# Cross-attention and a quantised feed-forward block on one core: statistics of two row blocks moved to DVE, unread products between two stages, another order of loads, and one early set of scores

## The chip, the core and the metric

The kernel runs on one core of a Trainium2 chip. The core has a matrix engine (TensorE, PE in the profile; its weight loads are shown as PEld), a vector engine (VectorE, DVE), a scalar engine (ScalarE, ACT), a general engine (GpSimd, POOL) and SyncE (SP), which only issues DMA transfers here. Each engine has its own queue of instructions, which it works through in order. Engines wait for one another by semaphores. The metric is the device time of one execution in microseconds, lower is better; the time given for a kernel is the median of its runs.

## The reference

The input x has 2 x 2048 rows of 512 numbers, so 4096 rows; a context of 128 rows belongs to each half.

```python
x = x + xattn(layernorm(x), ctx, Wq, Wkv)          # softmax(q k^T / sqrt(512)) v
h = layernorm(x)
x = x + ffn(h, w_gate, w_up, w_down)

# ffn: every act_qdq rounds to 16 bits by ONE scale, the largest |value| of the whole tensor / 32767
h    = act_qdq(h)
up   = act_qdq(h @ lpbq(w_up).T)                    # 512 -> 1536; lpbq: 4-bit weights, blocks of 32
gate = act_qdq(h @ lpbq(w_gate).T)
sig  = round(sigmoid(gate) * 65536) / 65536
p    = act_qdq(gate * sig)
o    = act_qdq(p * up)
out  = o @ lpbq(w_down).T                           # 1536 -> 512
```

Four of these scales need the largest value of a whole tensor (h, gate, up, o) before the next step can round anything. That cuts the work into stages.

## The kernel before

Rows are worked on in 8 groups of 512 (`NG`, `TG`), each of 4 blocks of 128 rows (`NJ`). The stages are attention, gate, up, and down.

**Attention (lines 268 to 521).** A loop over i = 0..8 works on several groups at once. For a group g, `front` transposes x on PE (copied out of PSUM by ACT into `xT`) and takes mean and variance with DVE's `bn_stats`; `scores` multiplies by the folded keys (16 products), reduces the maximum on DVE and takes four exponentials on ACT; `turn` transposes these, and for the last group DVE copies the result to `eT`; `attend` multiplies by the values (`po`) and adds to x on DVE, with the row sum as a by-product; `normalise` takes the squares of x minus its mean on ACT (L463, with an accumulator read each), the inverse root on POOL (`pow`, L295), and writes the normalised `h` on ACT (L474). `abs_max` gathers the largest |h| (`hmax`), and `lift` transposes h on PE, copied by ACT to `hT` (L486). The last group has nothing beside it but the `lift` of group 6: its four blocks go through `normalise` one at a time. When all maxima are there, `over_partitions_by_pe` reduces `hmax` to one column (`m_h`), turns it on PE (`rows_h`), and reduces again: `a_h`. From it come the scale of h, the integers of group 0 (`first_integers`), and the first gate product (L547).

**Gate and up (lines 588 to 831).** An integer of 16 bits is split into parts that the matrix engine multiplies exactly. One output chunk takes 8 products into `q` and 4 into `e`. Gate results and up results go to DRAM (`gate_d`, `up_d`); during up, p is computed and stored too (`p_d`). Tiles are stored by group in reversed order, so up's last tiles (group 0) remain in the three buffers `tiles_u`, with their p in `kept_p`.

**Between up and down (lines 835 to 994).** The maximum of up goes the same way as that of h: `m_u`, `rows_u` on PE (the pool `ps_m`, tag q), `a_u`. ACT rounds three candidates for the largest product (L850), DVE multiplies each with its p (L852, `product_b`), POOL reduces them over partitions (`top`), and a flag tells whether the largest |o| is known by this. Every engine reads the flag (L993) and branches (L994) over a slow path, which isn't taken here. `round_up` (L903, ACT) rounds up's rows of tile 0 in the meantime.

**Down (lines 1044 to 1094).** Here a tile t has 256 rows (`TD`; two tiles to a group, `NS` = 2), and a step m is a block of 128 rows (two to a tile, `NU` = 2; j is the block in the tile). Step m runs: `round_o` on DVE (`oi`, `sa`, a part of `o_parts`) and its cast on ACT (L929), `third_part` on DVE, 24 products `yq` and 12 products `ye` on PE. Two steps later ACT evacuates the first sum (L953), POOL adds x (L955), DVE adds the second sum (L959, `finish`), and SP stores the rows (L961). The roundings of the next tile, `round_up(uis[t + 1], t + 1)`, are three instructions on ACT. They are put behind the casts of the step j = 0. After the first tile of a group, `load_up` brings the next group's up from DRAM into `tiles_u` (three transfers of 1 MB, L877, traced at the same step); they can start when the rounding of that group's second tile has read the buffers. `load_p` brings p of a tile in six transfers of 128 KB (L887, two buffers), traced two steps before its use, for tiles 2 to 15; tiles 0 and 1 have `kept_p`. `load_x1` brings the rows to which the result is added (L894).

**What sets the order.** The framework plans the queue of each engine itself. It takes the instructions in the order in which the program traces them, as a priority, but picks one that its own timing model calls ready before one that it calls waiting; memory comes from pools with a fixed number of buffers. `tc.high_priority()` puts what is traced in it ahead of everything else that is ready. `in_order(a, b, ...)` fixes that b stands behind a where both are on one engine's queue, without a wait. On each queue the planned order then holds on the chip.

Of the kernel before, what the change touches and what calls it, by code (L numbers as in the profile page):

```python
# [49 lines left out]
F32 = mybir.dt.float32  # L50
# [6 lines left out]
AF = mybir.ActivationFunctionType  # L57
# [6 lines left out]
P = 128  # L64
# [12 lines left out]
def tile_xattn_ffn(  # L77
# [67 lines left out]
    def over_partitions_by_pe(pool, tag, shape, stats, name):  # L145

        m = const.tile([P, 1], F32, name=f"m_{name}")
        nc.vector.tensor_reduce(m, stats, AX.X, ALU.max)
        rows = pool.tile(shape, F32, tag=tag, name=f"rows_{name}")
        rows = rows[:, 0, :P] if len(shape) == 3 else rows[:, :P]  # L150
        nc.tensor.transpose(rows, m.to_broadcast([P, P]), ident)
        a = const.tile([P, 1], F32, name=f"a_{name}")
        nc.vector.tensor_reduce(a, rows, AX.X, ALU.max)
        return a

    def act_scale(a, name, unit=None):

# [110 lines left out]
    with ExitStack() as c0:  # L268

        with ExitStack() as c1:  # L270
# [185 lines left out]
            def normalise(g, js, h, total, nmean, squares, ve, rstd):  # L456
# [16 lines left out]
                for j in js:  # L473
                    nc.scalar.activation(  # L474
                        h[:, j, :], xt[:, j, :], AF.Identity, bias=nmean[:, j : j + 1], scale=rstd[:, j : j + 1]
                    )

            def lift(g, h):

                for j in range(0, NJ, 2):  # L480
                    pt = two_banks(f"ht_{g}_{j}")
                    pt4 = pt.rearrange("p (c j k) -> p c j k", c=ND, j=2)
                    for i in range(2):
                        for c in range(ND):
                            nc.tensor.transpose(pt4[:, c, i, :], h[:, j + i, ts(c, P)], ident)
                    nc.scalar.copy(hT[:, :, ds(g * TG + j * P, 2 * P)], pt.rearrange("p (c k) -> p c k", c=ND))  # L486
# [4 lines left out]
            for i in range(NG + 1):  # L491
                if i + 2 < NG:
                    xts[i + 2] = load_x(i + 2)
                if i:
                    eT, rden = turn(i - 1, soft[0]), soft[1]
                    hs[i - 1] = wk2.tile([P, NJ, D], F32, tag="h", name=f"h_{i - 1}")
                    rows = row_stats(i - 1)
                if 0 < i < NG:
                    soft = scores(i, *ahead)
                    advance(gate_steps, 2)  # L500
                    attend(i - 1, range(NJ), eT, rden, rows[0])
                    nc.sync.dma_start(out=x1_d[i - 1], in_=xts[i - 1])
                if i == NG:
                    for j in range(NJ):
                        attend(i - 1, [j], eT, rden, rows[0])
                    for j in range(NJ):
                        normalise(i - 1, [j], hs[i - 1], *rows)
                        abs_max(hmax[:, i - 1 + j : i + j], hs[i - 1][:, j, :])
                    nc.sync.dma_start(out=x1_d[i - 1], in_=xts[i - 1])
                if i + 1 < NG:  # L510
                    ahead = front(i + 1)
                    advance(gate_steps, 2)
                if i > 1:
                    lift(i - 2, hs.pop(i - 2))
                if 0 < i < NG:
                    normalise(i - 1, range(NJ), hs[i - 1], *rows)
                    abs_max(hmax[:, i - 1 : i], hs[i - 1], AX.XY)
                advance(gate_steps, 2)
            advance(gate_steps, 100)
            lift(NG - 1, hs.pop(NG - 1))  # L520
            a_h = over_partitions_by_pe(ps_o, "o", [P, D], hmax, "h")


        wp_late = ctx.enter_context(tc.tile_pool(name="wp_late", bufs=NF - NE))
# [140 lines left out]
    with ExitStack() as c3:  # L665
# [166 lines left out]
        in_order(stored, *rest)  # L832


        a_u = over_partitions_by_pe(ps_m, "q", [P, 2, TG], umax, "u")

        r_u = const.tile([P, 1], F32, name="r_u")
        nc.vector.tensor_scalar(r_u, a_u, 1.0 / QMAX, tiny_u, ALU.mult, ALU.max)
# [9 lines left out]
        for i, (uv, pv) in enumerate([*there, (ub, pb)]):  # L848
# [4 lines left out]
            if i == 0:  # L853
                nc.vector.tensor_scalar(most[:, 3:4], best[:, 1:2], r_u, 1.0 + 2.0**-18, ALU.mult, ALU.mult)
                nc.vector.tensor_scalar(most[:, 3:4], most[:, 3:4], 0.5 * (QMAX + 2.0), None, ALU.add)
        top = const.tile([P, 4], F32, name="top")
        nc.gpsimd.partition_all_reduce(top, most, P, bass_isa.ReduceOp.max)


    with ExitStack() as c5:  # L860
# [12 lines left out]
            return ts(j, 2)  # L873

        def load_up(g):
            for k in range(NK):
                nc.sync.dma_start(  # L877
                    out=tiles_u[k].rearrange("p (h c) t -> p h c t", h=2),
                    in_=up_d[rows_of(g, k)].rearrange("h p c t -> p h c t"),
                )  # L880

        def load_p(t):
            pi = ld.tile([P, NF, TD], I16, tag="p5", name=f"p5_{t}")
            for k in range(NK):
                for h in range(2):
                    c = 2 * order.index((groups[t // NS], k)) + h
                    nc.sync.dma_start(  # L887
                        out=pi[:, ds(NQ * k + 2 * h, 2), :], in_=p_d[c, :, :, ts(t % NS, TD)]
                    )
            return pi  # L890

        def load_x1(t):
# [157 lines left out]
        for m in range((last + 1) * NU + 2):  # L1050
# [4 lines left out]
            if m <= last * NU + NU - 1:  # L1055
# [27 lines left out]
                if m == 0:  # L1083
                    scale_of_o()
                    in_order(casts[-1], *round_up(ui, 0, P, P))
                if j == 0 and t < last:
                    uis[t + 1] = up_integers(t + 1)
                    in_order(casts[-1], *round_up(uis[t + 1], t + 1))
                    if t % NS == NS - 2 and t + NS <= last:
                        load_up(groups[t // NS + 1])  # L1090
            if m > 1:
                stored = finish(m - 2, qx, e)
                if m - 2 < last * NU + NU - 2:
# [24 lines left out]
```

## Time and profile before

| | |
|---|---|
| median of 3 runs | 994.45 us (994.12 to 996.3) |
| the profiled execution | 997.23 us, span 995.4 us |
| mean granted PE clock | 0.981 |
| PE busy | 942.0 us (95%), 4322 instructions |
| PEld busy | 764.5 us (77%) |
| DVE busy | 804.8 us (81%), 999 instructions |
| ACT busy | 547.3 us (55%), 654 instructions |
| POOL busy | 87.2 us (9%), 66 instructions |
| DMA | 263.72 MB, mean 265 GB/s |

In the profile a line names the line of the kernel (L903), the engine, the operation, and what is written from what is read (`ui<-u`). The rows of 40 digits cut the span into 40 slices of 24.9 us; a digit is the busy share of an engine in tenths, and for PEclk the clock that PE was granted. A timeline row has its start in us, the busy time of the group, the engine and the line, how many instructions it merges (x4), and in square brackets how long the engine had idled before it and for what. A row of waits has the total, the number of waits and the longest. The chain of work that ended last is followed back from the last instruction and shown in order of time.

### The profile page before, as it was taken

To read this page: it belongs to the slowest core of one execution; us is meant where nothing else is said; L and a number is where in the kernel's file an instruction comes from. 1 tells how busy PE (TensorE), PEld (TensorE's weight loads), DVE (VectorE), ACT (ScalarE), POOL (GpSimd) and SP (SyncE) were. 2 spreads that over 40 slices of the span, in tenths; PEclk is the share of its full clock that TensorE was granted. 3 is DMA by queue.
4 is the path that set the end of the run, shared out by engine and by line. 5 is a ranking of instruction groups with operands and counts; after the bars stand their busy time and mean duration, and the time that the engine had idled before them with its cause. 6 is when DMAs were issued, how large, how long until landed. Compare 5 with 4: busy or idle time off the path is not lost. (4 is left out here: it accounts for less than half of the span.)

```text
span 995.4 us, 11700 instructions
## 1 busy us (share of the span) xinstructions
PE 942.0 (95%) x4322; PEld 764.5 (77%) x4322; DVE 804.8 (81%) x999; ACT 547.3 (55%) x654; POOL 87.2 (9%) x66
## 2 busy tenths in 40 slices
PE   6998886999999999999999999999598999999998
PEld 6765654888878888878788888877486888888886
DVE  4579876898998999456898888969799988888882
ACT  2277788433233323218998999895445544444331
POOL 0101111000000000000000000000111222222221
PEclk9999897999999999999999999999899999999999
DMA  9187554967895965797997989969787656654711
GB/s 348 33 307 285 222 216 187 404 246 290 334 383 195 342 224 180 256 386 264 362 332 301 382 294 376 393 247 400 297 269 279 206 176 239 237 200 155 249 64 42
DMA packets 103596, 263.72 MB, mean 265 GB/s; under 512 B 6064, under 2 KB 46000, under 8 KB 94832
## 3 DMA queue, kind: packets, MB, share of 16 engines
q1 hardware_dynamic: 102496, 259.02, 70.2%
q0 software_dynamic: 512, 2.88, 0.8%
q10 hardware_dynamic: 528, 1.05, 0.3%
q8 instruction: 34, 0.56, 0.2%
q14 instruction: 26, 0.21, 0.1%
HBM read 136.05 MB, written 126.88 MB: 264 GB/s over the span
## 5 line engine op out<-in xcount | busy, mean ns | idle before, releaser
L547 PE MATMUL q_g<-parts_g,wg 128*128 128x512 f32 x768 | 195.3, 396 | 3.8 <-ACT parts_g L567 2.6
L547 PEld LDWEIGHTS q_g<-parts_g,wg 128*128 128x128 f32 x768 | 145.1, 190 | 34.3 <-ACT parts_g L567 3.0
L635 ACT ACTIVATE g<-q_g 128x512 f32<-128x512 f32 x96 | 57.3, 599 | 171.1 <-PE q_g L547 163.8
L547 PE MATMUL q_u<-parts_u,wu 128*128 128x512 f32 x576 | 142.5, 389 | 1.9 <-ACT u L799 1.4
L547 PEld LDWEIGHTS q_u<-parts_u,wu 128*128 128x128 f32 x576 | 108.0, 188 | 25.1 <-ACT u L799 2.7
L940 PE MATMUL yq<-wd,o_parts 128*128 128x512 f32 x512 | 121.7, 390 | 0.0
L940 PEld LDWEIGHTS yq<-wd,o_parts 128*128 128x128 f32 x512 | 96.7, 189 | 20.3
L553 PE MATMUL e_g<-parts_g,wg 128*128 128x512 f32 x384 | 103.2, 390 | 0.0
L636 DVE CUSTOM_DVE_ANT_0 g<-g,e_g 128x512 f32<-128x512 f32 x96 | 64.4, 679 | 43.1 <-PE e_g L553 39.7
L953 ACT ACTIVATE yqs<-yq,q_o 128x512 f32<-128x512 f32 x32 | 22.0, 687 | 127.6 <-PE yq L940 127.6
L553 PEld LDWEIGHTS e_g<-parts_g,wg 128*128 128x128 f32 x384 | 71.9, 188 | 14.9
L955 POOL TENSOR_TENSOR qx<-yqs,x 128x512 f32<-128x512 f32 x32 | 61.6, 1926 | 210.0 <-ACT yqs L953 165.5
L940 PE MATMUL yq<-first_wd,o_parts 128*128 128x512 f32 x256 | 66.5, 404 | 13.1 <-ACT o_parts L929 13.1
L553 PE MATMUL e_u<-parts_u,wu 128*128 128x512 f32 x288 | 77.0, 389 | 0.0
L932 DVE SCALAR_TENSOR_TENSOR o_parts<-sa,oi 128x1536 fp32r<-128x1536 int16 (+2 forms) x41 | 58.6, 1448 | 21.4 <-PE ye L948 21.4
L800 DVE TENSOR_TENSOR u<-u,e_u 128x1024 f32<-128x1024 f32 x47 | 56.9, 1217 | 17.4 <-ACT u L799 17.4
L928 DVE SCALAR_TENSOR_TENSOR o_parts<-sa,oi 128x1536 fp32r<-128x1536 int16 (+2 forms) x41 | 59.5, 1451 | 13.8 <-PE yq L940 12.3
L940 PEld LDWEIGHTS yq<-first_wd,o_parts 128*128 128x128 f32 x256 | 49.7, 195 | 24.2 <-ACT o_parts L929 13.7
L741 DVE CUSTOM_DVE_ANT_0 ua<-ua,pi 128x1024 f32<-128x1024 f32 x46 | 56.0, 1219 | 12.3 <-ACT ua L740 12.2
L948 PE MATMUL ye<-wd,o_parts 128*128 128x512 f32 x256 | 63.2, 389 | 0.0
L553 PEld LDWEIGHTS e_u<-parts_u,wu 128*128 128x128 f32 x288 | 54.0, 188 | 11.3
L733 DVE SCALAR_TENSOR_TENSOR pi<-gi,k_p,sq 128x2048 int16<-128x2048 int16 x24 | 56.4, 2348 | 4.8 <-ACT sq L694 4.5
(193 smaller groups left out, 1544.7 us busy)
## 6 DMA issues: line engine op xcount, KB each, us to landing
gate_d<-g SPq DMA_DIRECT2D x24, 1024.0 KB, 7.2
up_d<-u SPq DMA_DIRECT2D x48, 512.0 KB, 9.1
gt<-gate_d SPq DMA_DIRECT2D x22, 1024.0 KB, 8.7
u<-up_d SPq DMA_DIRECT2D x21, 1024.0 KB, 6.5
parts_d<-parts_g SPq DMA_DIRECT2D x6, 3072.0 KB, 11.8
parts_u<-parts_d SPq DMA_DIRECT2D x6, 3072.0 KB, 15.6
p_d<-pi SPq DMA_DIRECT2D x24, 512.0 KB, 10.2
p<-p_d SPq DMA_DIRECT2D x84, 128.0 KB, 3.2
```

What stands on the lines that cost most here:

```text
L547: nc.tensor.matmul(q, lhsT=w[:, s, c, :], rhs=parts[:, s, c, :], start=(c + s == 0), stop=(c + s == ND))
L553: nc.tensor.matmul(e, lhsT=w[:, 2, c, :], rhs=parts[:, 2, c, :], start=(c == 0), stop=(c == ND - 1))
L635: evacuated = nc.scalar.activation(g4[:, i, :], q, AF.Copy, scale=1.0 + 1.0 / BASE)
L636: subtracted = nc.vector.tensor_tensor_reduce(g4[:, i, :], g4[:, i, :], e, 1.0, LOWEST, ALU.subtract, ALU.max, gtop[:, m : m + 1])
L733: nc.vector.scalar_tensor_tensor(pi, gi, k_p, sq, ALU.mult, ALU.mult)
L741: nc.vector.tensor_tensor_reduce(ua, ua, pi, 1.0, 0.0, ALU.mult, ALU.max, pumax[:, c : c + 1])
L800: less = nc.vector.tensor_tensor(u4[:, both, :], u4[:, both, :], e, ALU.subtract)
L928: made.append(nc.vector.scalar_tensor_tensor(parts[1][:, c], sa[:, c], -BASE, oi[:, c], ALU.mult, ALU.add))
L932: return nc.vector.scalar_tensor_tensor(parts[2][:, c], sa[:, c], BASE + 1.0, oi[:, c], ALU.mult, ALU.subtract)
L940: nc.tensor.matmul(q, lhsT=parts[s][:, f, :], rhs=wd[f][:, s, :], start=(f + s == 0), stop=(f + s == NF))
L948: nc.tensor.matmul(e, lhsT=parts[2][:, f, :], rhs=wd[f][:, 2, :], start=(f == 0), stop=(f == NF - 1))
L955: nc.gpsimd.tensor_tensor(qx, qs, x1[:, m % NU, :], ALU.add)
```

## The change

There are four edits.

1. In the last group's normalisation, blocks j = 2 and 3 go through a new helper, `normalise_by_dve`, which takes mean and variance with `bn_stats` and `bn_aggr` on DVE, where `normalise` takes the squares on ACT. The inverse root stays on POOL and the write of `h` on ACT.
2. The scores of the last group are traced at high priority.
3. Between up and down PE gets six f32 products of the identity with 512 columns, behind `rows_u`. Five read the first quarter of the last up tile, the sixth the third `product_b`. Nobody reads their result.
4. In down, the first loads of p (tile 2) are put behind the first `load_up` on SP; and from tile 1 on, the roundings of the next tile stand behind the casts of the step j = 1 instead of j = 0, and the `load_up` of the later groups is traced there too. For t = 0 both stay at j = 0.

```diff
-        nc.tensor.transpose(rows, m.to_broadcast([P, P]), ident)
+        turned = nc.tensor.transpose(rows, m.to_broadcast([P, P]), ident)
...
-        return a
+        return a, turned
...
+            def normalise_by_dve(g, js, h, total, nmean, squares, ve, rstd):
+
+                xt = xts[g]
+                for j in js:
+                    st = sm.tile([P, 6], F32, tag="st", name=f"sth_{g}_{j}")
+                    nc.vector.bn_stats(st, xt[:, j, :])
+                    mv = sm.tile([P, 2], F32, tag="mvh", name=f"mvh_{g}_{j}")
+                    nc.vector.bn_aggr(mv, st)
+                    at = slice(j, j + 1)
+                    nc.vector.tensor_scalar(ve[:, at], mv[:, 1:2], EPS, None, ALU.add)
+                    inverse_root(rstd[:, at], ve[:, at])
+                    nc.vector.scalar_tensor_tensor(nmean[:, at], mv[:, 0:1], -1.0, rstd[:, at], ALU.mult, ALU.mult)
+                    nc.scalar.activation(h[:, j, :], xt[:, j, :], AF.Identity, bias=nmean[:, at], scale=rstd[:, at])
...
-                    soft = scores(i, *ahead)
+                    if i < NG - 1:
+                        soft = scores(i, *ahead)
+                    else:
+                        with tc.high_priority():
+                            soft = scores(i, *ahead)
...
-                        normalise(i - 1, [j], hs[i - 1], *rows)
+
+                        (normalise if j < NJ // 2 else normalise_by_dve)(i - 1, [j], hs[i - 1], *rows)
...
-        a_u = over_partitions_by_pe(ps_m, "q", [P, 2, TG], umax, "u")
+        a_u, turned = over_partitions_by_pe(ps_m, "q", [P, 2, TG], umax, "u")
...
+        unread = ps_m.tile([P, 2, TG], F32, tag="e", name="unread")[:, 0, :]
+        idle = [
+            nc.tensor.matmul(unread, lhsT=ident, rhs=v, start=True, stop=True)
+            for v in [u4[:, 0, :]] * 5 + [product[:, :TG]]
+        ]
+        in_order(turned, *idle)
...
         def load_up(g):
-            for k in range(NK):
+            return [
                 nc.sync.dma_start(
...
+                for k in range(NK)
+            ]
...
-                    nc.sync.dma_start(
+                    load = nc.sync.dma_start(
                         out=pi[:, ds(NQ * k + 2 * h, 2), :], in_=p_d[c, :, :, ts(t % NS, TD)]
                     )
+
+                    if t == NS:
+                        in_order(up_loads[-1], load)
...
-                if j == 0 and t < last:
+                if j == (0 if t == 0 else NU - 1) and t < last:
                     uis[t + 1] = up_integers(t + 1)
                     in_order(casts[-1], *round_up(uis[t + 1], t + 1))
                     if t % NS == NS - 2 and t + NS <= last:
-                        load_up(groups[t // NS + 1])
+                        up_loads = load_up(groups[t // NS + 1])
```

## The prediction

> **What bounds the kernel now.** I read the page first: PE is busy for 95% of the span, and its only weak slices are the first seven (up to about 170 us) and slice 29 (716 to 741 us).
>
> ```profile
> PE   6998886999999999999999999999598999999998
> ...
> DVE  4579876898998999456898888969799988888882
> ACT  2277788433233323218998999895445544444331
> ...
> PEclk9999897999999999999999999999899999999999
> ```
>
> Between the weak places PE runs without pause: from 165 to 700 us its waits add up to under 8 us. So time can only be won before the first gate product (167.29 us), in the gap between up and down (711 to 722 us), and wherever down has a gap. The chain of work that ended last shows the third place.
>
> ```profile
> 740.39 0.63 ACT o_parts L929
> 741.02 0.26 SPq L877
> 741.37 9.96 DMA u<-up_d
> 751.38 1.03 issue
> 752.41 0.61 ACT o_parts L929
> 753.06 7.34 PE yq L940 x24
> 760.40 2.72 PE ye L948 x12
> 763.12 5.44 PE yq L940 x24
> ```
>
> From 753.06 on the chain is PE alone, 8.16 us a block of 128 rows (24 + 12 matmuls), up to the end. The block at 753.06 took 7.34 us for its first sum in place of 5.44. The waits of 725 to 760 us name what held it:
>
> ```profile
> ACT ui L903 <- DMA u<-up_d: 6.2, 3, 3.6
> PEld yq L940 <- ACT o_parts L929: 4.6, 1, 4.6
> PE yq L940 <- ACT o_parts L929: 4.2, 1, 4.2
> ```
>
> ACT runs in order: three roundings of tile 2's up rows (L903) stand before the casts of block 3, and they wait for up's tiles, which SP issued behind ten loads of p:
>
> ```profile
> 732.90 7.22 SPq L887 DMA_DIRECT2D p<-p_d  x10
> 740.23 1.56 SPq L877 DMA_DIRECT2D u<-up_d  x3
> ```
>
> For the end of attention I read the timeline. ACT is the engine without gaps; it idles 0.69 + 0.17 + 0.43 = 1.3 us in all from 141.74 to 163.03, and the last normalisation hangs on it:
>
> ```profile
> 158.31 0.70 ACT L463 ACTIVATE h<-xt,row 128x512 f32<-128x512 f32 x1
> ...
> 159.72 1.89 ACT L486 COPY hT<-ht 128x1024 f32<-128x1024 f32 x2
> ...
> 161.51 1.52 ACT L474 ACTIVATE h<-xt,row,row 128x512 f32<-128x512 f32 x2
> ...
> 167.29 6.67 PE L547 MATMUL q_g<-parts_g,wg 128*128 128x512 f32 x16 [2.64 <-ACT parts_g L567]
> ```
>
> The profiled execution took 997.23 us (span 995.4), 2.78 above the median of the runs, 994.45; I sum against the former and take 2.78 off at the end.
>
> **The change, part by part.**
>
> *Statistics of rows 2 and 3 of the last group by DVE.* Removed from ACT: two squares (0.716 us median) with their accumulator reads (0.190): 1.81 us of an engine that has no gap between them and the last normalisation. Added to DVE: two bn_stats (0.663) and two aggregates (0.166), 1.66 us; the small adds, multiplies and POOL's powers (0.54) stay about as many. DVE's last attend ends at 154.75 and it then idles 1.23 us before 157.02 and more before 160.4, so the statistics fit; were that cover gone they cost their 1.66. The last normalisation ends 4.26 us before the first gate product, so what ACT gains there the product gains. Ends: -3.7 (the two 0.95 us copies of group 6 also fall behind the normalisations, as nothing would keep these waiting) and 0 (DVE late by what ACT saves). I take **-1.8**, what the two squares cost.
>
> *Scores of group 7 at high priority.* No work is added. The 16 products (PE 137.81 to 141.55) could start at 136.8, when xT has been copied; the four exponentials, now split 142.63 and 146.62 by 2.93 us of group 5's normalisation, would stand together, and eT (149.04) could come up to 2 us sooner. ACT's sum of work is unchanged, so the gain is bounded by its 1.3 us of idle time. The other end: eight transposes that feed a copy go behind, 1.0 us lost. I take **-0.7**, near the idle time's half.
>
> A displaced start of the gate products also moves against the clock: it read 0.50 from 159.6 to 173.1 us, so 5.8 us of products ran at half speed (some 2.9 us lost). A shorter or longer cold stretch adds up to 1.2 us either way; I take 0.
>
> *The six unread products.* Each f32 product of 128x512 is two instructions 0.43 us apart at full clock (attention's po, L445): five fill about 713.4 to 717.7, the sixth waits for the third test product (718.80) and ends by 719.8, before the branch (720.4) and the first cast (722.2); behind it on PE stand only the branch and block 0. At half clock they would end near 723.6. The clock now falls to 0.50 at about 715.9 and is back at 726.1, so PE loses about 1.95 us on block 0. But block 1 starts at 732.22, when ACT's first cast for it is done (it stands behind six roundings, 726.60 to 731.67), and a faster block 0 still ends at 731.4. So the cover is those roundings, and PE itself was 0.2 us late at most. I take **-0.2**; ends -1.95 and +0.3.
>
> The Trainium skill's page "TensorE: Matmul & The Clock Gate", Part 1, says that an idle window of about 3.4 us halves the clock and a busy one restores it. That agrees with the fall at 715.9 and the return at 726.1, and read alone it would credit these products with the whole 1.95 us, a sum of -8.3. The chain of the trace puts DVE and ACT on the path there, so I keep -0.2.
>
> *Up's tiles ahead of p's, and rounding one block later.* Now block 3's casts no longer stand behind the roundings. Its `sa` (746.25, first piece) and `o_parts` (747.34) are ready when PE ends block 2 at 748.75. The whole 4.15 us of idle time and the 1.9 us of cold clock behind it vanish: 6.05. What is late next is block 4. Its rounding now stands behind the third cast of block 3: `sa` ends 750.27, cast 0.62, three roundings of 1.15: 754.35 (now 752.5). From the start of `oi` to the end of the cast block 4 took 753.46 to 758.33, 4.87 us (`oi` 1.80, `sa` 1.44, cast 1.48). 754.35 + 4.87 = 759.2 against PE's present start of block 4, 762.96: 3.7 us won, and 4.6 if `sa` takes 0.56 us as it does at 889.86 where POOL is silent. PE would wait about 2.3 us before block 4 (748.75 + 8.16 = 756.9). Block 5 then follows: DVE needs 7.5 us a block against 8.16.
>
> The queues: SP still has 12 loads of p at 0.6 to 0.7 us each, up's three (0.4) and x1's two. If up's go out at once (732.9) they land by about 742; if six loads of tile 3's p slip in ahead, 737.2 and about 747; both are before 750.9. The p of tile 2 then goes behind up's: issued by 743 and, with the slowest landing of 10.8 us, there by 754. If up's stay at 740.2, p is issued by 746 and there by 757 at worst: 757 + 4.87 = 761.9, only 1.1 won. POOL's queue waits for nothing new. In the later groups loads and rounding move together by one block, 8.16 us: now a group's loads are out at 888.5 and its rounding is due at 901.2, about 5 us after landing, and that distance stays. DVE idles 0.58 + 0.96 us a block there, which covers a later `ui`. Ends -6.05 and -1.1; I take **-3.9**, nearest to the rows of block 4.
>
> Sum: -1.8 - 0.7 - 0.2 - 3.9 = -6.6. 997.23 - 6.6 = 990.6; less 2.78, **987.8 us**.
>
> **The rivals.** About 2 us (0.2%) is what a measurement of this kernel can tell from no change.
>
> *The stall moves to block 4.* p of tile 2 or the rounding is late (the 1.1 above), attention still gains: -3.8, 990.6 us. For it: SP's 7.22 us for ten loads of p. Against: 754 is the worst landing if up's loads go out soon.
>
> *Everything gains.* DVE ends block 3 sooner, so the 6.05 come whole, and attention reaches -3.7: about -10, 984.5 us. Against: DVE had no idle time from 728.55 to 753.46.
>
> *Attention gives it back.* The new order costs about what down gains (statistics late on DVE, transposes behind the scores, a longer cold stretch): within 2 us of now, about 994 us.
>
> *Slower.* Up's loads of the later six groups are held on SP, in order, behind `out` and p loads that wait for DVE; ACT then waits in the rounding with the casts behind it, and PE stalls at each group. It costs once a load is over 5 us later than now; it decides against the change from 1.4 us a group on (6 x 1.4 = 8.4). With 1.8 us a group, 998.6 us. For it: SP's wait for ACT's L903 is already up to 5.7 us long with everything queued behind. Against: PE's lead over its casts is about 9 us in steady blocks (cast ends 891.65 + 1.47, due 901.5).
>
> **How the numbers follow.** Forecast (985.5 to 990): 0.54. Stall at block 4 (990 to 992.5 mostly): 0.16. Everything gains: 0.10. Given back: 0.09. Slower: 0.11. Faster by over 0.2%: 0.54 + 0.13 + 0.10 = 0.77; within: 0.11 (0.09 and the rest of block 4's); slower: 0.12 with the worst of giving back. The range leaves out the lower part of "everything gains" and most of "slower": 984.5 to 996.5.
>
> **What would show it.** Right: the first gate product near 165 us; a clock near 1.00 through the gap between up and down with the first down product still some 11 us after up's last; no wait of PE for a cast before block 3, one of 1 to 3 us before block 4, and 8.16 us a block from there. In SP's order u<-up_d stands ahead of most p<-p_d. Wrong: a first gate product at 167 or later, waits of ACT's L903 for DMA at several groups, or block 4 starting after 761 us less what came before. What would upset it most is an order of SP or ACT that I cannot read from this trace.

## The result, and the profile after

The changed kernel took 997.63 us (median of 20 runs, 994.20 to 1001.75) where the kernel before took 994.14 us (20 runs, 992.25 to 996.38). The ratio is 1.0035, with a 95% interval of 1.0024 to 1.0045: slower by 3.5 us. The forecast was 987.8 us, and the time lies above the range of 984.5 to 996.5. The profiled execution of the changed kernel took 996.3 us (span 994.5, mean granted clock 0.986).

The page of the changed kernel, the span in 40 slices:

```profile
PE   6997886999999999999999999999889999999998
...
DVE  4589877898998999546898888978799999988882
ACT  2278778533233333227998999896354454443431
...
PEclk9999897999999999999999999999989999999999
```

PE's weak place near 715 us reads 8 and 8, where it read 5 and 9, which the unread products alone could do. The first seven slices, the attention, are the same but for one tenth. A page in tenths shows neither a gain nor a loss of 4 us, so I follow four points of time through all profiled executions: the copy of the last group's x (ACT L307, the last thing in common before the edits of attention), the first gate product, `rows_u`, and the end. The table gives the time between them in us, each from one profiled execution, with the end taken from the span, which is given to 0.1 us.

| kernel | x copied to first gate product | first gate product to rows_u | rows_u to the end |
|---|---|---|---|
| before, first profile | 32.37 | 545.78 | 282.33 |
| before, second profile | 33.03 | 546.54 | 278.46 |
| changed, first profile | 35.45 | 546.21 | 278.93 |
| changed, second profile | 35.18 | 548.27 | 280.46 |

Attention became 2 to 3 us longer. Down did become shorter against the first profile of before, but not against the second. The middle stage, which no edit touches, took between 544.1 and 552.3 us over all seventeen profiles; this spread was not attributed, and it is why single executions are compared here stage by stage.

The waits of the changed kernel that answer to those shown of before (total, number, longest, in us):

```profile
PEld yq L972 <- ACT o_parts L961: 5.0, 2, 3.1
PE yq L972 <- ACT o_parts L961: 3.7, 2, 2.2
```

The rows for ACT's rounding waiting for up's tiles, 6.2 us before, are gone. Of PE's 3.7 us, 2.2 stand before block 0. The rest stands in the chain of work that ended last:

```profile
752.75 1.21 DVE sa L958
753.96 0.02 issue
753.98 0.62 ACT o_parts L961
754.61 3.14 ACT ui L935 x3
757.75 0.02 issue
757.77 1.83 DVE oi L957
...
760.28 1.48 ACT o_parts L961
761.76 0.04 issue
761.80 5.83 PE yq L972 x24
767.63 2.72 PE ye L980 x12
770.35 5.44 PE yq L972 x24
```

Here the reader sees the new place of the stall: the three roundings (L935) stand behind block 3's third cast (753.98), DVE's `oi` waits for them, and PE starts block 4 at 761.80, 46.23 us after `rows_u`, having waited 1.47 us. SP's queue shows that the loads did move as the diff says:

```profile
733.74 1.62 SPq L904 DMA_DIRECT2D u<-up_d  x3
735.41 8.74 SPq L916 DMA_DIRECT2D p<-p_d  x6
```

So the order of loads and roundings went as forecast, and the time did not.

### The profile page after: what moved, and what is told of

The parts are those of the page before. It is cut to its first block, busy times and chain, and to the rows that moved or that the text cites. A ratio compares the mean times of both kernels' runs of the same rounds, so it can differ in the third digit from the quotient of the medians.

```text
span 994.5 us, 11724 instructions
## 1 busy us (share of the span) xinstructions
PE 946.4 (95%) x4334; PEld 766.9 (77%) x4334; DVE 813.2 (82%) x1001; ACT 546.8 (55%) x650; POOL 88.5 (9%) x66
## 3 DMA queue, kind: packets, MB, share of 16 engines
q0 software_dynamic: 512, 2.88, 0.8%
## 5 line engine op out<-in xcount | busy, mean ns | idle before, releaser
L961 ACT CAST o_parts<-sa 128x1536 fp32r<-128x1536 int16 (+2 forms) x41 | 48.8, 1192 | 58.1 <-DVE sa L958 57.0
L964 DVE SCALAR_TENSOR_TENSOR o_parts<-sa,oi 128x1536 fp32r<-128x1536 int16 (+2 forms) x41 | 61.1, 1509 | 13.1 <-PE ye L980 13.1
L960 DVE SCALAR_TENSOR_TENSOR o_parts<-sa,oi 128x1536 fp32r<-128x1536 int16 (+2 forms) x41 | 59.6, 1454 | 9.1 <-PE yq L972 6.6
```

Of the source, the lines that this page charges most:

```text
L960: made.append(nc.vector.scalar_tensor_tensor(parts[1][:, c], sa[:, c], -BASE, oi[:, c], ALU.mult, ALU.add))
L961: return made, nc.scalar.copy(parts[0][:, c], sa[:, c])
L964: return nc.vector.scalar_tensor_tensor(parts[2][:, c], sa[:, c], BASE + 1.0, oi[:, c], ALU.mult, ALU.subtract)
```

## The experiments

All comparisons are with runs of the kernel before on the same chip.

**The kernel before, once more.** No edit.

> The kernel before, for a second profiled execution. Theory 3, the 4.15 us that PE waited before block 3 in the first profile is that execution's (it took 2.8 us more than the median, and two unchanged down stages in the runs above waited 1.2 and 2.4 us there): a wait of 1 to 2.5 us before block 3, and block 5 some 54.5 us after the turned maximum of up instead of 58.05. Against theory 3: a wait near 4 us again.

Measured: 993.57 us, span 991.8. Block 3 starts 37.20 us after `rows_u` and block 4 at 45.68. The timeline of this execution, ACT and PE:

```profile
743.81 1.15 ACT L903 ACTIVATE ui<-u,r_u 128x1024 int16<-128x1024 f32 x1 [0.52 <-DMA u<-up_d]
...
746.35 1.15 ACT L903 ACTIVATE ui<-u,r_u 128x1024 int16<-128x1024 f32 x1 [1.40 <-DMA u<-up_d]
...
748.83 1.15 ACT L903 ACTIVATE ui<-u,r_u 128x1024 int16<-128x1024 f32 x1 [1.33 <-DMA u<-up_d]
...
750.54 2.14 PE L940 MATMUL yq<-first_wd,o_parts 128*128 128x512 f32 x8 [1.26 <-ACT o_parts L929]
```

ACT waits for up's tiles here too, but 3.2 us in all and not 6.2, and PE 1.26 us and not 4.15, as theory 3 had it (block 5 follows 54.15 us after `rows_u`); the clock stays at 1.00. The six other profiles with before's order in down (the runs below with the scores, the statistics, the exponentials behind the squares, the unread products, rows_h ahead, and the maximum left out) have 1.20 to 2.37 us at block 3, with the clock full. The long wait, and the cold clock behind it (a granted clock of 0.50), stand in one profile of eight: the one the forecast was made from, whose 997.23 us lay 2.78 above its median and above the longest of before's 20 runs in the result, 996.38.

**Only the edits of down.**

```diff
+                    if t == NS:
+                        in_order(up_loads[-1], load)
...
-                if j == 0 and t < last:
+                if j == (0 if t == 0 else NU - 1) and t < last:
```

> The kernel before with only the new order of down (up's tiles ahead of p's, rounding one block later). Theory 1, the loss lies in attention (the profile after has its first gate product at 169.36 us against 167.29, and block 4 of down 3.7 us earlier measured from up's end): this alone gains about 3.7 us, near 990.5, with runs as close together as those of before. Theory 2, the loss lies in down, in executions that the profile did not catch (runs of the changed kernel spread from 994 to 1002): this alone loses 2 to 4 us in the median and has the spread.

Measured: 997.26 us, ratio 1.0027 (1.0014 to 1.0040). Block 4 starts 46.05 us after `rows_u`, after a wait of 2.05 us, and its first sum takes 7.42 us. Three windows of the profile say why (us; then length, busy time of PE, PEld, DVE, ACT, POOL; then the granted clock):

```profile
760.00:762.00 2.00, 0.08 (x1) 0.08 (x1) 1.89 (x2) 1.60 (x2) 0.00 (x0) 1.00 0.00 0
762.00:764.00 2.00, 2.00 (x7) 1.56 (x8) 2.00 (x3) 0.46 (x1) 1.47 (x1) 0.78 0.00 0
764.00:766.00 2.00, 2.00 (x6) 1.52 (x6) 2.00 (x2) 0.00 (x0) 0.98 (x1) 0.50 0.03 6
```

PE is idle up to 761.92, works, and at about 763.1 the clock falls to one half for 3.4 us. In the first profile of the changed kernel the same windows show no fall:

```profile
760.00:762.00 2.00, 0.53 (x3) 0.19 (x1) 1.89 (x3) 1.72 (x2) 0.00 (x0) 1.00 0.00 0
762.00:764.00 2.00, 2.00 (x9) 1.59 (x9) 2.00 (x3) 0.34 (x1) 1.58 (x1) 1.00 0.00 0
764.00:766.00 2.00, 2.00 (x10) 1.64 (x10) 2.00 (x2) 0.00 (x0) 0.87 (x1) 1.00 0.03 8
```

Ten products against six in the last window. What follows: the edits of down didn't win 3.9 us; here they cost 2.7, within what theory 2 had.

**Only the scores at high priority.**

```diff
+                        with tc.high_priority():
+                            soft = scores(i, *ahead)
```

> The kernel before with only the last group's scores at high priority. Theory 1: attention's last products and transposes change places on PE, ACT idles about 3 us more between 137 and 151 us, and this alone costs 2 to 3 us, near 996.5. Theory 2: within 1 us of the kernel before.

Measured: 998.70 us, ratio 1.0042 (1.0027 to 1.0058), and 36.46 us from the copy of x to the first gate product in place of 32.37 and 33.03 in the two profiles of before. This edit alone costs 4.2 us by the medians, more than the 2 to 3 of theory 1. ACT's timelines of the kernel before, from the fourth square of group 5 on, and of the changed kernel, from the third, show the way; L463 are the squares of group 5, L338 the exponentials of group 7, L474 the write of the normalised rows of group 5:

```profile
141.13 0.72 ACT L463 ACTIVATE h<-xt,row 128x512 f32<-128x512 f32 x1
...
142.63 0.46 ACT L338 ACTIVATE e<-sc,nmx,rstd 128x128 f32<-128x128 f32 x1 [0.69 <-DVE nmx L334]
...
143.79 2.93 ACT L474 ACTIVATE h<-xt,row,row 128x512 f32<-128x512 f32 x4 [0.17 <-DVE row L472]
146.62 0.44 ACT L338 ACTIVATE e<-sc,nmx,rstd 128x128 f32<-128x128 f32 x1
```

```profile
138.88 0.71 ACT L463 ACTIVATE h<-xt,row 128x512 f32<-128x512 f32 x1
...
139.88 0.46 ACT L338 ACTIVATE e<-sc,nmx,rstd 128x128 f32<-128x128 f32 x1 [0.20 <-DVE nmx L334]
...
141.63 1.93 ACT L500 COPY hT<-ht 128x1024 f32<-128x1024 f32 x2
...
143.43 0.76 ACT L463 ACTIVATE h<-xt,row 128x512 f32<-128x512 f32 x1
...
145.92 2.93 ACT L474 ACTIVATE h<-xt,row,row 128x512 f32<-128x512 f32 x4 [1.65 <-DVE row L472]
```

The four exponentials and two copies of `hT`, some 3.9 us, went between the third square of group 5 and the fourth. The inverse root needs all four squares, so ACT idles 1.65 us before the normalisation, where it idled 0.17, and groups 5 and 6 follow late. From the copy of x to `m_h`, the column of the maxima, ACT's gaps add up to 5.3 us in the run with this edit alone, and to 1.3 and 2.2 in the two profiles of before. Before, the four squares stood together from 139.00, and the exponentials were the ones that were split.

**Only the statistics.**

```diff
-                        normalise(i - 1, [j], hs[i - 1], *rows)
+                        (normalise if j < NJ // 2 else normalise_by_dve)(i - 1, [j], hs[i - 1], *rows)
```

> The kernel before with only the statistics of two row blocks on DVE. Theory 1: ACT loses 1.8 us of work, but the last transposes now wait for copies that fall behind the last normalisations, and the turned maximum stands behind them on PE: between -1 and +1.5 us. Theory 2: within 1 us of the kernel before. If the order that the planner gives gate's instructions after it matters, the gate stage itself will differ by more than 1 us.

Measured: 994.49 us, ratio 0.9999 (0.9987 to 1.0011), and 31.58 us from the copy of x to the first gate product (32.37 before). The maximum `m_h` came 27.30 us after the copy of x, where it had been 28.87: 1.57 us were won. But `rows_h` followed `m_h` by 1.21 us and no longer by 0.43. Why is taken up below.

**The changed kernel again, on the chip of these three.**

> The changed kernel once more, for another profiled execution. Both theories: 996 to 1000 us, median 3 to 4 us above the kernel before. Theory 1: attention ends some 2 us later whatever the execution. Theory 2: an execution near 1000 us shows waits of PE in down, after block 4, that the first profile lacks.

Measured: 1001.22 us (6 runs), ratio 1.0063 (1.0043 to 1.0083), 6.7 us above before, where both theories had 3 to 4. Its profile has both losses, the late first gate product (35.18 us) and a cold block 4 (2.15 us of wait, 7.45 us for the first sum); in the first profile block 4 was not cold.

**Only up's loads ahead of p's** (the first of the two hunks of down).

> The kernel before with only up's loads ahead of p's; the rounding stays behind block 2's casts. Theory 3: the late rounding is what holds block 4 in the new down (46.05 to 46.23 us after the turned maximum, often with a cold clock behind it), and up's tiles now land before ACT reaches block 3's casts: no wait before block 3, one of under 1.5 us before block 4, block 5 at 52.5 to 53.5 us, 1 to 2 us faster than before. Rival: DVE, not the rounding, holds block 4: block 5 at 54.5 us or later, no gain.

Measured: 995.16 us, ratio 1.0001 (0.9987 to 1.0014). PE does not wait before block 3 any more, as forecast; it waits 0.86 us before block 4 instead, at 45.57. Block 5 starts at 54.00, between the 52.5 to 53.5 of the theory and the 54.5 of the rival, and the 1 to 2 us of the theory were not won: ACT has waited 5.05 us for DVE's `sa` before it can cast for block 4, so DVE's chain is what PE waits for there.

**Only the later rounding** (the second hunk).

> Of the change only the later rounding: the roundings of the next tile behind the casts of the step j = 1 from tile 1 on, with the loads of up still behind those of p. Theory (this half of the third edit is what costs in down): block 4 waits for the three roundings behind block 3's third cast, as it did with both halves; no wait of over 0.3 us at block 3, 1.4 to 2.5 us at block 4, block 4 at 46 to 47 us after rows_u, and the time 2 to 3.5 us above before (ratio 1.002 to 1.0035). Rival (the cost needs the order of the loads too): block 4 below 45.9 us after rows_u and the time within 1 us of before.

Measured: 994.70 us, ratio 0.9994 (0.9978 to 1.0010). Block 4 starts at 45.20 after 1.25 us of waiting. The theory missed: a rounding behind the third cast is not late by itself. It took both halves together to bring block 4 to 46.1. What differs is a coincidence of POOL and DVE. With both halves (the run of the two edits of down):

```profile
752.63 1.30 POOL L986 TENSOR_TENSOR qx<-yqs,x 128x512 f32<-128x512 f32 x1 [9.52 <-ACT yqs L984]
752.88 1.20 DVE L957 TENSOR_SCALAR sa<-oi 128x512 int16<-128x512 int16 x1
```

With the later rounding alone:

```profile
753.40 0.29 DVE L957 TENSOR_SCALAR sa<-oi 128x512 int16<-128x512 int16 x1
...
755.62 1.84 POOL L986 TENSOR_TENSOR qx<-yqs,x 128x512 f32<-128x512 f32 x1 [11.99 <-DMA out<-qx]
```

With before's order of loads the store `out` of an earlier block leaves SP late, POOL's addition to block 2 waits for it, and block 3's third `sa` takes 0.29 us. With up's loads first, the store leaves early, POOL adds at once, and the same `sa`, begun 0.25 us after the addition, takes 1.20 us, to 0.15 us past the addition's end. It is so in all profiles: this `sa` takes 1.19 or 1.20 us in the seven with up's loads first, and 0.29 or 0.30 in the ten with before's order. The Trainium skill's page "SBUF — State Buffer", section "SBUF: two separate sides", says that POOL and DVE, in some forms of its instructions, share a pair of ports which the one that starts first keeps for its whole instruction. These rows agree with it; which form `sa` takes, no run here shows.

**Both halves, with one addition of POOL left out.** For block 1, ACT writes the scaled sum straight to `qx`; the x of those rows is left out.

```diff
-            qs = wk2.tile([P, D], F32, tag="qs", name=f"yqs_{m}")
...
             qx = wk2.tile([P, D], F32, tag="qx", name=f"qx_{m}")
+            if m == 1:
+                return nc.scalar.activation(qx, q, AF.Copy, scale=q_o), qx
```

> Both halves of the third edit alone, and for block 1 of down the addition of x on POOL is left out: ACT writes the scaled first sum straight to qx, so x is missing from the rows of block 1. Theory (POOL's addition holds block 3's third sa, and through the cast and the roundings it holds block 4): that sa takes 0.29 us in place of 1.20, block 4 starts at 45.0 to 45.5 us after rows_u in place of 46.1, PE waits under 1.5 us for it and its first 24 products take under 5.8 us; the time is within 1.2 us of before (ratio 0.9988 to 1.0012). Rival (the addition only stands beside it; the later rounding or the p loads cost the time): block 4 at 45.9 us or later, or the time 2 us and more above before as without this.

Measured: block 4 at 45.22, a wait of 1.28 us, 5.83 us for its first sum (the theory had under 5.8); 995.79 us, ratio 0.9997 (0.9982 to 1.0013). The start of block 4 came as the theory has it, but by another `sa` than it named:

```profile
742.29 0.30 DVE L957 TENSOR_SCALAR sa<-oi 128x512 int16<-128x512 int16 x1
...
751.96 1.29 POOL L988 TENSOR_TENSOR qx<-yqs,x 128x512 f32<-128x512 f32 x1 [13.45 <-ACT yqs L987]
752.21 1.19 DVE L957 TENSOR_SCALAR sa<-oi 128x512 int16<-128x512 int16 x1
```

The addition at the third `sa` of block 3 is that of block 2, and it was still there. The one taken away, of block 1, had fallen on block 2's second `sa` (1.20 us at 742.06 with both halves, here 0.30). It lies in the same chain of DVE, and its 0.9 us reached block 4 in full. In the kernel before it falls there too (1.20 us), so it is no part of what the change costs. So it is shown that such a coincidence delays block 4; that the other one does the same follows from the rows of the two kernels above, and was not taken away by itself.

**Both halves again, on that chip.**

> Both halves of the third edit alone, as in the first run of that kind, on the chip of the run with the addition left out. Theory: third sa of block 3 1.20 us, block 4 at 46.0 to 46.3 us, wait of 1.4 to 2.3 us, and the time 1.5 to 3.5 us above before (ratio 1.0015 to 1.0035). Rival: within 1 us of before, so that the first measurement of these two together was the chip's own.

Measured: 996.13 us, ratio 1.0005 (0.9988 to 1.0022). Block 4 started at 46.23 with a wait of 1.18 us and a full clock. The third `sa` of block 3 took 1.19 us, as forecast. The rival held as far as the time goes: on this chip the two edits cost 0.4 us, on the first 2.7. This profile is that of the fastest of the 12 runs, 992.36 us. Block 0's first sum took 8.64 us in it, in place of 7.55 in the first run of both halves, so that PE came later to block 4, whose start ACT and DVE set, and waited less. The two intervals overlap between 1.0014 and 1.0022.

**The scores, with their exponentials behind the squares of group 5.** High priority stays; one order is added.

```diff
+                if g == NG - 1:
+                    in_order(squared[NG - 3], exps[0])
```

> Only the last group's scores at high priority, but its first exponential kept behind group 5's last square on ACT. Theory 1 (with the scores early, group 5's fourth square stands behind four exponentials and two copies, and its inverse root leaves ACT idle; all later work follows): the cost falls from 4.2 us to under 1.5 us, first gate product at 167 to 168.5 us. Rival (the products ahead of group 4's transposes on PE cost the time): it stays at 3 to 4 us.

Measured: 994.71 us, ratio 0.9996 (0.9979 to 1.0013), 33.00 us from the copy of x to the first gate product. ACT's timeline:

```profile
139.48 1.93 ACT L505 COPY hT<-ht 128x1024 f32<-128x1024 f32 x2
141.29 0.73 ACT L468 ACTIVATE h<-xt,row 128x512 f32<-128x512 f32 x1
...
142.01 0.46 ACT L339 ACTIVATE e<-sc,nmx,rstd 128x128 f32<-128x128 f32 x1
...
144.36 2.93 ACT L479 ACTIVATE h<-xt,row,row 128x512 f32<-128x512 f32 x4 [0.48 <-DVE den L349]
```

The fourth square is back in front of the exponentials, and the cost of 4.2 us is gone; ACT's gaps up to `m_h` are 2.1 us again. The two copies of `hT` still stand between the third square and the fourth. So the exponentials in front of the fourth square were the cause, and not the score products on PE, which start 1.04 us after the copy of x in this run as in the run with the scores alone (2.88 in before); early scores by themselves are worth nothing measurable.

**Only the unread products.** Nothing reads what they compute.

> Only the six unread products. Both theories: nothing (within 1 us); the clock is again 0.50 when down's first products start, since 2 us pass between the last unread product and them, and ACT's roundings hide it.

Measured: 994.86 us, ratio 0.9997 (0.9983 to 1.0012). PE's timeline of the changed kernel:

```profile
715.70 4.46 PE L879 MATMUL unread<-u,ident 128*128 128x512 f32 x10
721.44 1.12 PE L879 MATMUL unread<-product_b,ident 128*128 128x512 f32 x2 [1.28 <-DVE most L871]
724.80 3.78 PE L972 MATMUL yq<-first_wd,o_parts 128*128 128x512 f32 x8 [2.23 <-ACT o_parts L961]
```

They shorten PE's idle time before block 0 from 8.93 to 2.23 us, and it doesn't show. The clock was at 0.50 again when block 0 began, as expected: from 722.98 us on in this run, block 0 from 723.03.

**The change without the scores.**

> The changed kernel without the high priority of the last group's scores. Theory (the costs add: 4.2 from the scores, 2.7 from down, nothing from the statistics and the unread products): first gate product at 166 to 168 us, block 4 waits 1.4 to 2.5 us, and the time is 2 to 3.5 us above before (ratio 1.002 to 1.0035). Rival (the edits bear on one another, as a cold start of block 0 or a shift of the clock's windows does): within 1 us of before, or 4 us and more above it.

Measured: 996.32 us, ratio 1.0014 (0.9995 to 1.0032); first gate product 32.37 us after the copy of x, block 4 after a wait of 2.18 us and cold. By its profile it is what the theory says; by its time, 0.9 us above before, it falls into the rival's band, and the interval holds both. It is inconclusive on whether the costs add; it fits that the scores are most of the change's loss.

**The statistics, with rows_h ahead.** The maxima are turned before the last lift is traced, so that `rows_h` stands on PE in front of six of its sixteen transposes.

```diff
-            lift(NG - 1, hs.pop(NG - 1))
             a_h, _ = over_partitions_by_pe(ps_o, "o", [P, D], hmax, "h")
+            lift(NG - 1, hs.pop(NG - 1))
```

> Of the change only the statistics by DVE, and with them rows_h traced ahead of the last lift, so that on PE it stands in front of six of the last transposes. Theory (with the statistics on DVE, rows_h is held by those transposes, 1.2 us behind m_h): rows_h within 0.3 us of m_h, first gate product at 165.5 to 166.5 us in place of 167.4, the time about 1 us below before (ratio 0.998 to 0.9997). Rival (the last copy of hT on ACT, or the clock, holds the first product next): first gate product at 166.8 to 168 us and the time within 0.7 us of before.

Measured: 994.40 us, ratio 0.9988 (0.9972 to 1.0005). `rows_h` followed `m_h` by 0.73 us, and the first gate product came 32.38 us after the copy of x: the rival, by this profile. By its median, 1.0 us below before, the time is the theory's, but the interval reaches past 1. And here the clock was at 0.50 from 151.4 to 154.8 us, when the attend products ran, and DVE waited for them; the second profile of before, cold from 149.8 to 153.2, has 33.03 us. The same order of attention was profiled once more in the version at the end of this section, with a full clock there.

**The same, with group 6's maximum left out of the scale** but for one column.

```diff
-                    abs_max(hmax[:, i - 1 : i], hs[i - 1], AX.XY)
+                    if i < NG - 1:
+                        abs_max(hmax[:, i - 1 : i], hs[i - 1], AX.XY)
+                    else:
+                        abs_max(hmax[:, i - 1 : i], hs[i - 1][:, 0, :1])
```

> As the run with rows_h ahead, and the largest |h| of group 6 is taken over one column of it only: this part of the maximum is left out of the scale, and with it 2.1 us of DVE. Theory (DVE is what the statistics lengthen: its five absolute maxima stand back to back, 4.65 us, in front of m_h, and the two squares taken from ACT cannot show): m_h at 161 to 162 us in place of 163.1, first gate product at 163.8 to 165.2 us, the time 2 to 3.5 us below before (ratio 0.9965 to 0.998). Rival (ACT's order or POOL's powers hold m_h as much as DVE does): m_h after 162.5 us and less than 1 us won beside the run with rows_h ahead.

Measured: 993.52 us, ratio 0.9978 (0.9962 to 0.9995). DVE's timeline of the kernel before, of the changed kernel, and of this one:

```profile
157.02 3.47 DVE L180 TENSOR_REDUCE hmax<-h 128x1 f32<-128x2048 f32 x3 [1.23 <-ACT h L474]
...
162.36 1.39 DVE L180 TENSOR_REDUCE hmax<-h 128x1 f32<-128x512 f32 x2 [0.49 <-ACT h L474]
```

```profile
159.52 4.66 DVE L180 TENSOR_REDUCE hmax<-h 128x1 f32<-128x2048 f32 x5 [0.59 <-ACT h L474]
164.22 0.17 DVE L148 TENSOR_REDUCE m_h<-hmax 128x1 f32<-128x11 f32 x1
```

```profile
157.52 2.80 DVE L180 TENSOR_REDUCE hmax<-h 128x1 f32<-128x512 f32 x4
160.35 0.17 DVE L148 TENSOR_REDUCE m_h<-hmax 128x1 f32<-128x11 f32 x1
```

In the changed kernel all five maxima stand back to back in front of `m_h`; before they were two lots, 3.47 and 1.39 us, with 1.9 us between. Without the long one `m_h` came at 160.35, 26.50 us after the copy of x (28.30 in the run before it). The first gate product, at 165.76, missed the theory's 165.2, and the gain, 1.9 us, its 2. Beside the run with `rows_h` ahead 0.9 us were won by the medians, and 0.47 us at the first gate product by the profiles, less than the 1 us that the rival allowed. DVE's maxima are what holds `m_h` once the statistics are on DVE, but little of it reached the gate; behind `m_h` the copies of `hT` on ACT come next (162.79 and 164.18, between the roundings of `hi`).

**A version put together from what cost nothing:** statistics by DVE with `rows_h` ahead, and the later rounding alone.

> A version put together from what cost nothing: statistics by DVE with rows_h ahead of the last transposes, and the later rounding without the other order of loads; no high priority, no unread products. Theory (the gains add: 0.5 to 1 us each by medians): 1 to 2 us below before (ratio 0.998 to 0.999), block 4 at 45.0 to 45.4 us after rows_u. Rival (neither was a gain beyond the measurement): within 0.7 us of before.

Measured: 994.47 us, ratio 0.9989 (0.9974 to 1.0004); block 4 at 45.21. In its profile `m_h` comes 27.30 us after the copy of x, `rows_h` 0.22 us behind it, and the first gate product at 30.93, 1.44 us sooner than in before's first profile. The median is 1.2 us below before, as the theory has it, but the interval reaches past 1, so no gain is shown. It is well below the changed kernel.

## Why the prediction was wrong

- **The base.** "The whole 4.15 us of idle time and the 1.9 us of cold clock behind it vanish: 6.05." They did vanish, but they weren't there in an ordinary execution: the second profile of before has 1.26 us and no cold clock, and six others with before's order in down have 1.20 to 2.37. I then took the 2.78 us by which the profiled execution lay above its median off at the end, as if they lay elsewhere. The stall was what set that execution apart in down (282.33 us there against 278.46), so it was counted twice. This is the step that failed first.
- **Block 4, -3.9 us.** The start of the block came out: 759.2 is 46.1 us after `rows_u`, and five profiles with both halves have 46.05 to 46.23. But that is luck, for two sizes in the working were off by 0.9 us and cancel: block 3's third `sa` was given 0.29 us and took 1.20, and block 4 was given 4.87 us from `oi` to the end of its cast and took 3.99, with an `sa` of 0.56 in place of 1.44. And the kernel before usually reaches block 4 at 45.7 and not at 49.9, so the same 46.1 is 0.4 us of loss. On top comes the clock. With both halves it fell at block 4 in three of five profiles, whose down took 280.3 to 280.5 us; in the other two down took 278.9. Against 278.46 in the second profile of before, that is 1.9 us with the fall and 0.4 without, where the medians of the two measurements say 2.7 and 0.4. The three executions with the fall lie 0.2 to 2.7 us above the median of their kernel, the two without it 1.3 and 3.8 below, so how often it falls is not known. I had written of 0.9 us more if `sa` is slow beside POOL, but for the long `sa` of block 4, and didn't see that the order of loads sets when POOL adds.
- **The scores, -0.7 us, ends -1.3 and +1.0.** It cost 4.2 by itself. I bounded the gain by ACT's idle time and the loss by transposes on PE. What I left out is that exponentials that come earlier on an engine in order push something else back: here the one square that a normalisation waits for, with 1.65 us of new idle time behind it. ACT's present 1.3 us of idle time bounds what can be won, but not what can be lost: the four exponentials take 1.75 us, and in front of that square they cost more than twice as much. The rival "attention gives it back" named the stage and about the price, what down was to gain; only, down had nothing to set against it.
- **The statistics, -1.8 us.** At `m_h` 1.57 us were won, near the estimate. The error was to let the first gate product follow `m_h`: `rows_h` had been 0.43 us behind it and fell behind the last transposes on PE, 1.21 and 2.00 us in the profiles of the statistics alone and of the change without the scores. With `rows_h` ahead, one profile shows 1.44 us at the first gate product. "The statistics fit" was wrong as well: DVE had gaps for them, but its five maxima then stand in one row in front of `m_h`.
- **The unread products, -0.2 us.** Nothing contradicts it: 0.9997, with an interval from 1.7 us less to 1.2 us more. The cover that the prediction named, ACT's roundings, is there: in nine profiles block 0's first sum took 7.22 to 7.39 us, and block 1 starts 19.16 or 19.17 us after `rows_u` in all of them, 0.17 us ahead of the first profile of before. But the run does not test what a full clock would do, for it was at half speed when block 0 began (its first eight products took 3.78 us in the changed kernel, as in before).
- **The rival "slower"** reached 998.6 us by another mechanism, up's later loads held on SP. ACT's rounding waits for no load at all in the changed kernel, so that mechanism is out; the sign was right for reasons it doesn't name.
- **The signs in the section on what would show it** were good ones: "a first gate product at 167 or later" was given as wrong, and it came at 169.36; the clock was to stay near 1.00 through the gap between up and down, and it fell to 0.50 at 723.5 us; the wait of 1 to 3 us before block 4 was there.
- **Two readings of the trace** were off without entering the sum: the weak slice of the first page spans 697 to 722 us, not 716 to 741, and PE's lead over its casts in steady blocks is 8.4 us by the two numbers given, not 9.

The parts measured alone, 4.2 us for the scores, 0.4 to 2.7 for down and nothing measurable for the other two, add up to 4.6 to 6.9 us, where the change cost 3.5 and 6.3.

What stays open: how often the clock falls at block 4, how much of the change's 3.5 to 6.3 us on two chips is that, whether the costs add, and the spread of gate and up.

## What to carry to other kernels

A stall that one profile shows is worth what it costs in an ordinary execution: where the profiled one lies 0.3% above its median, look for the excess in the very stall that is to be removed, and take a second profile of the kernel before first. Work that is moved ahead on an engine in order pushes something back, and can cost more than its own length, so look for whoever collects several results from that engine, such as a root that needs all four squares, and price the wait for the last of them. And a milestone won on one engine (`m_h` here) is a gain only when the next step on the next engine has a free place in its queue.

## What the runs showed of the hardware

- POOL's addition of 128x512 in f32 (1.28 to 1.30 us) stretched a DVE `tensor_scalar` of 128x512 int16 from 0.29 to between 1.19 and 1.24 us in every profile where the latter began 0.20 to 0.25 us after it. Without the addition the same instruction took 0.30 us. Where it began 0.26 us ahead of the addition, in the changed kernel's block 2, it kept its 0.29, and the DVE instruction behind it took 1.70 us in place of 0.69. An order of DMA loads decided whether they met.
- The clock fell to 0.50 for 3.4 us after PE had waited only 2.05, 2.15 or 2.18 us before block 4, and stayed full after 1.47, 1.18 and 0.86 us there and after 2.00 and 2.37 us before block 3. The traces show what the difference is. In all 17 profiles the stretches between two changes of the clock last whole multiples of 3.41 us, so the changes lie on a grid of that step, which lies elsewhere against the kernel in each execution. From the first gate product on, 3995 steps of this grid ran at full clock. By PE's records, it idled 1.99 us or more in each of the 23 steps before a fall, and 1.88 us or less in each of the 3972 others. The waits before block 4 after which the clock fell lay in one step but for 0.05 us at most (2.05, 2.10 and 2.18 us); those of 2.00 and 2.37 us before block 3 were split by a border (at most 1.34 and 1.81 us in one step). This was read out of the traces afterwards, and no run was made to test it. It does not hold in attention, where the clock fell after steps with 1.12 us of idle time, among transposes of 128 columns.
- The Trainium skill's page "TensorE: Matmul & The Clock Gate", Part 1, has an idle window of about 3.4 us, free-running, before the clock is halved. The step and the free position agree with these traces; that some 2.0 us of idle time in a window were enough does not follow from the page, and here the measurement decides.
- The cold stretches near the end of attention, too, lay elsewhere from profile to profile: 159.6 to 173.2 us in before's first, and three between 151.4 and 171.9 in the first run with `rows_h` ahead, the earliest of which cost that run's attend products their speed.
